# A two-layer graph attention kernel on one core: every map product as 64x64 array tiles, scores and values alternating step by step

## The chip, the core and the metric

One core of a Trainium2 chip runs the kernel. Its engines are TensorE (PE; its weight loads are shown as PEld), VectorE (DVE), ScalarE (ACT), GpSimd (POOL) and SyncE (SP), which issues most transfers. SBUF is the working memory, PSUM the accumulators that TensorE writes. The metric is the device time of one execution in microseconds; the kernel before takes 2929.03 us (median of 3 runs, 2928.76 to 2929.57).

## What is computed

Eight graphs share one adjacency matrix of 2048 x 2048 nodes; each node has 64 features. The reference, cut to its core:

```python
mask = graph + jnp.eye(N) > 0
h = jnp.einsum('bnc,hdc->bhnd', x, Wh)              # B=8, N=2048, H=4 heads of D=64
out_h = gat(h)     # scores h.h^T, masked, softmax over m, times h, plus bias bh
z = leaky_relu(concat(out_h), 0.2)
h2 = jnp.einsum('bnk,dk->bnd', z, Wo)               # 256 -> 64
out2 = gat(h2)                                      # one head, bias bo
z2 = leaky_relu(out2, 0.2)
out = layernorm(z2) * gamma + beta
return layernorm(x + out)
```

Everything is float32. The two attention layers make (32 + 8) score maps of 2048 x 2048.

## The kernel before, in words

`gat_kernel` runs `fast_kernel`, which subtracts a fixed shift in the exponent instead of a row maximum, sums all row sums into a flag, and runs `general_kernel` only if a sum left its safe range; no profile here shows the second.

`fast_kernel` works in 20 **units**. A first-layer unit (16 of them) is one batch element with two heads; a second-layer unit (4) is a pair of batch elements with the one head of layer two. In both, the two maps (j = 0, 1) lie on partitions 0-63 and 64-127 of `hT` (transposed) and in the two column halves of `hN` (plain, with the bias added). A unit has four **chunks** c of 512 columns and each chunk 16 **steps** m of 128 rows:

- `scores` (L525): for j = 0, 1 one matmul `hT[rows j, 128 of m]` x `hT[rows j, 512 of c]` into a PSUM tile of the pool "s" (L529); VectorE subtracts the mask into an SBUF tile `e` (L532), ScalarE takes the exponent in place (L534). Because the maps are symmetric, `e` holds the transposed attention.
- `values` (L537): for j = 0, 1 one matmul `hN[:, m, half j]` x `e[:, j]`, accumulated over the 16 steps in one PSUM tile `o` (L541).
- `add_up` (L544): POOL adds the `e` of steps 0 to 12 into `acc` (L550, L554); the last three (`DIRECT`) stay as they are.
- `sums` (L559): the row sums `pz` by matmuls with a vector of ones from `acc` and the three tiles, four 32-column tiles at once (L569); ScalarE copies them out (L572), transfers lay them out as `zt` (L578); the leaky relu of `o` follows on ScalarE and VectorE (L582, L583). `invert` (L586): reciprocal on VectorE, out to HBM and back as a broadcast (`rd`, `z`). `scale` (L598): `o` times `z`. `project` (L601): in layer one the product with `woT` (L608), added up over heads in `h2T`; in layer two the product with a centring matrix (L616) and `norm1`, and a period later `norm2` (L620 to L656): both layer norms, nearly all on VectorE, with the power -0.5 on POOL (L628).
- `prepare` (L498): the maps of the next unit: `ph` = `whT` x `xT` (L510), copied to `hT`, and `pn`, its transposes (L520), into `hN`.

TensorE can work as tiles: a matmul of 64 rows uses half of the rows of its array, one of 64 columns half of the columns. The score matmuls here are 64x128 tiles, two side by side; the value matmuls 128x64, two side by side; the row sums 128x32, four. A float32 matmul shows in the trace as two records.

The program order is written out by hand (`manual_schedule`): each engine runs its instructions in the order in which the loop at the end calls them. The loop goes by **periods** of four steps: `scores` four times, then the row sums if due, then `values` four times and `add_up` four times for the period before, then other jobs that the table `jobs` holds for this period (mask building, the tail of an earlier chunk, preparing the next unit). `e` tiles come from a pool of 14, "s" tiles from 3 (two PSUM banks each), `o` from 2.

Of the kernel before, what the change touches and what calls it, by code (L numbers as in the profile page):

```python
# [26 lines left out]
F32 = mybir.dt.float32  # L28
I32 = mybir.dt.int32
BF16 = mybir.dt.bfloat16  # L30
AF = mybir.ActivationFunctionType
# [5 lines left out]
SLOPE = 0.2  # L37
FMAX = 3.4028234663852886e38

BIG = 1e16  # L40
# [313 lines left out]
def fast_kernel(ctx: ExitStack, tc: tile.TileContext, x, adj, Wh, bh, Wo, bo, gamma, beta, out, flag):  # L354
# [10 lines left out]
    BATCH = 4  # L365
    K = 2 * CB
    DIRECT = 3
# [3 lines left out]
    epool = ctx.enter_context(tc.tile_pool(name="epool", bufs=14))  # L371
    accs = ctx.enter_context(tc.tile_pool(name="accs", bufs=2))
    work = ctx.enter_context(tc.tile_pool(name="work", bufs=7))
    small = ctx.enter_context(tc.tile_pool(name="small", bufs=4))
    psum = ctx.enter_context(tc.tile_pool(name="psum", bufs=3, space=bass.MemoryType.PSUM))
# [9 lines left out]
    def opsum(name):  # L385
        return psum.tile([P, W], F32, tag="o", name=name, bufs=2)

    def wtile(name):
        return work.tile([P, W], F32, tag="w", name=name)

# [5 lines left out]
    identi = const.tile([P, P], I32, name="identi")  # L396
    nc.vector.tensor_copy(identi, ident)
# [21 lines left out]
    zall = const.tile([P, chunks, 8], F32, name="zall")  # L419

# [34 lines left out]
    mask = [const.tile([P, NB, W], BF16, name=f"mask{c}") for c in range(NC)]  # L455
# [7 lines left out]
    def mask_rows(c, g, st):  # L463
        if g // 2 == c:
            for k in range(2):
                r = 2 * (g % 2) + k
                d = st[:, r, k * P:(k + 1) * P]
                nc.gpsimd.tensor_tensor(d, d, identi, OP.add)
        m = work.tile([P, CB, 2 * P], BF16, tag="w", name=f"mrow{c}_{g}")
        nc.scalar.activation(m, st, AF.Relu, bias=shifts[:, 2:3], scale=-BIG)  # L470
        return m
# [15 lines left out]

    h2T = {}

    class Unit:  # L490
# [7 lines left out]
        def prepare(self, part):  # L498

            n, h = self.n, part % 2  # L500
            if part < 2:
                if self.second:
                    self.hT = h2T[self.bp]
                    return
                if h == 0:
                    self.hT = big.tile([P, N], F32, tag="hT", name=f"hT{n}")
                rows = slice(self.b2 * C, (self.b2 + 1) * C)
                p = spsum(f"ph{n}_{h}")
                for q in range(2):
                    nc.tensor.matmul(p[:, q * W:(q + 1) * W], whT[rows, self.hp * P:(self.hp + 1) * P],  # L510
                                     xT[self.bp][rows, (2 * h + q) * W:(2 * h + q + 1) * W], start=True, stop=True)
                nc.scalar.copy(self.hT[:, h * 1024:(h + 1) * 1024], p)  # L512
                return

            if h == 0:
                self.hN = big.tile([P, NB, P], F32, tag="hN", name=f"hN{n}")
# [8 lines left out]
        def scores(self, c, m):  # L525
            ps = spsum(f"s{self.n}_{c}_{m}")
            for j in range(2):
                rows = slice(j * D, (j + 1) * D)
                nc.tensor.matmul(ps[:, j * W:(j + 1) * W], self.hT[rows, m * P:(m + 1) * P],  # L529
                                 self.hT[rows, c * W:(c + 1) * W], start=True, stop=True)  # L530
            e = slot([P, 2, W], F32, f"e{self.n}_{c}_{m}")
            nc.vector.tensor_tensor(e, ps.rearrange("p (j i) -> p j i", j=2),  # L532
                                    mask[c][:, m, :].unsqueeze(1).to_broadcast([P, 2, W]), OP.subtract)
            nc.scalar.activation(e, e, AF.Exp, bias=shifts[:, 1:2] if self.second else shifts[:, 0:1], scale=1.0)  # L534
            return e

        def values(self, c, m, e):  # L537
            if m == 0:
                self.O[c] = opsum(f"o{self.n}_{c}")
            for j in range(2):  # L540
                nc.tensor.matmul(self.O[c][j * D:(j + 1) * D, :], self.hN[:, m, j * D:(j + 1) * D], e[:, j, :],  # L541
                                 start=(m == 0), stop=(m == NB - 1))

        def add_up(self, c, m, e):  # L544
# [7 lines left out]
            elif m < NB - DIRECT:  # L552
# [4 lines left out]


        def sums(self, c):  # L559
# [20 lines left out]

            o5 = wtile(f"o5{n}_{c}")
            nc.scalar.mul(o5, self.O[c], SLOPE)  # L582
            nc.vector.tensor_tensor(self.O[c], self.O[c], o5, OP.max)  # L583
# [14 lines left out]
        def scale(self, c):  # L598
            nc.vector.tensor_tensor(self.z[c], self.O[c], self.z[c], OP.mult)  # L599

        def project(self, c):  # L601

            z, p = self.z[c], self.O[c]
            if not self.second:
                if self.bp not in h2T:
                    h2T[self.bp] = big.tile([P, N], F32, tag="h2T", name=f"h2T{self.bp}")
                rows = slice(self.b2 * D, (self.b2 + 1) * D)
                nc.tensor.matmul(p[rows, :], woT[:, self.hp, :], z, start=True, stop=True)  # L608
                dst = h2T[self.bp][rows, c * W:(c + 1) * W]
                if self.hp == 0:  # L610
                    nc.scalar.copy(dst, p[rows, :])
                else:
                    nc.vector.tensor_add(dst, dst, p[rows, :])  # L613
                return
            for i in range(CB):
                nc.tensor.matmul(p[:, i * P:(i + 1) * P], z[:, i * P:(i + 1) * P],  # L616
                                 centre.rearrange("p r d -> p (r d)"), start=True, stop=True)
            self.norm1(c, p.rearrange("p (k d) -> p k d", d=D))

        def rstd(self, c, y, tag):  # L620

            n = self.n
            st = small.tile([P, 2, K], F32, tag="st", name=f"st{n}_{c}_{tag}")
            sq = wtile(f"sq{n}_{c}_{tag}").rearrange("p (k d) -> p k d", d=D)
            nc.scalar.square(sq, y)  # L625
            nc.vector.tensor_reduce(st[:, 0, :], sq, AX.X, OP.add)  # L626
            nc.scalar.activation(st[:, 1, :], st[:, 0, :], AF.Identity, bias=shifts[:, 3:4], scale=1.0 / D)  # L627
            nc.gpsimd.tensor_tensor(st[:, 0, :], st[:, 1, :], mhalf, OP.pow)  # L628
            return st[:, 0, :].unsqueeze(2).to_broadcast([P, K, D])

        def norm1(self, c, y):
            xr = wtile(f"xr{self.n}_{c}")
            xv = xr.rearrange("p (i b d) -> p i b d", b=2, d=D)
            for b2 in range(2):
                nc.sync.dma_start(out=xv[:, :, b2, :],
                                  in_=x[2 * self.bp + b2, c * W:(c + 1) * W, :].rearrange("(i p) d -> p i d", p=P))
            nc.vector.tensor_mul(y, y, self.rstd(c, y, 0))
            nc.vector.tensor_mul(y, y, gam.unsqueeze(1).to_broadcast([P, K, D]))
            nc.vector.tensor_add(y, y, bet.unsqueeze(1).to_broadcast([P, K, D]))
            nc.vector.tensor_add(y, y, xr.rearrange("p (k d) -> p k d", d=D))  # L640
            self.xr = xr
# [156 lines left out]
```

## Time and profile before

| | |
|---|---|
| runs | 2928.76, 2929.03, 2929.57 us |
| profiled execution | 2929.27 us, span 2927.8 us |
| mean granted TensorE clock | 0.977 |
| first score matmul of unit 0 | 29.2 us after the start |
| last score matmul | 54.0 us before the end |
| busiest group on POOL | L554, 880 adds, 2079.9 us |
| chain that ended last | PE 60%, ACT 14%, DVE 11%, transfers 5% |

The page's groups give, for each line and shape, the busy time (the union of its records), the mean duration of one, and the idle time of the engine just before them with what ended it. In the order of time a row is: start, length, engine, line, operation, tiles, shape, count, and in brackets the idle time ahead of it with its releaser. In the table by stage a row is: stage, its length, then busy time and count of PE, PEld, DVE, ACT and POOL, the granted clock, the share of the DMA engines and GB/s.

### The profile page before, as it was taken

To read this page: it belongs to the slowest core of one execution; us is meant where nothing else is said; L and a number is where in the kernel's file an instruction comes from. 1 tells how busy PE (TensorE), PEld (TensorE's weight loads), DVE (VectorE), ACT (ScalarE), POOL (GpSimd) and SP (SyncE) were. 2 spreads that over 40 slices of the span, in tenths; PEclk is the share of its full clock that TensorE was granted. 3 is DMA by queue.
4 is the path that set the end of the run, shared out by engine and by line. 5 is a ranking of instruction groups with operands and counts; after the bars stand their busy time and mean duration, and the time that the engine had idled before them with its cause. 6 is when DMAs were issued, how large, how long until landed. Compare 5 with 4: busy or idle time off the path is not lost.

```text
span 2927.8 us, 33405 instructions
## 1 busy us (share of the span) xinstructions
PE 2730.6 (93%) x12550; PEld 967.9 (33%) x12550; DVE 1799.2 (61%) x1861; ACT 1656.4 (57%) x1625; POOL 2331.8 (80%) x1025
## 2 busy tenths in 40 slices
PE   7999999999998999999998899999999999998884
PEld 3333333333332333333333233333333333333221
DVE  4666656666666666566666665666566666666564
ACT  5765556556554555655654555565565556555442
POOL 5778888788777887888876888888888888877774
PEclk9999999999999999999999999999999999999997
DMA  4300001000000000100000000010000000000001
GB/s 129 123 16 8 8 8 26 8 8 8 12 22 17 10 9 8 23 8 8 12 18 12 19 8 9 8 26 8 8 8 8 8 8 12 8 12 23 15 19 27
DMA packets 118220, 54.03 MB, mean 18 GB/s; under 512 B 91266, under 2 KB 107714, under 8 KB 118050
## 3 DMA queue, kind: packets, MB, share of 16 engines
q1 hardware_dynamic: 117250, 51.36, 6.6%
q8 instruction: 100, 1.64, 0.2%
q0 software_dynamic: 176, 0.26, 0.1%
q14 instruction: 70, 0.57, 0.1%
q10 hardware_dynamic: 624, 0.20, 0.0%
HBM read 46.60 MB, written 4.52 MB: 17 GB/s over the span
## 4 chain that ended last, share of the span: by engine, by line
PE 60%; ACT 14%; DVE 11%; DMA 5%; issue 4%; SPq 3%; POOL 2%; ACTq 0%; DVEq 0%; POOLq 0%
PE o L541 28%; PE s L529 25%; ACT e L534 11%; DVE e L532 6%; DMA zt<-zsb 4%; SPq L578 3%; PE ph L510 2%; PE o L608 2%; POOL st L628 2%; ACT zsb L572 1%; PE pn L520 1%; ACT o L582 1%; PE pz L569 1%; DVE hN L522 1%; DVE st L626 1%
## 5 line engine op out<-in xcount | busy, mean ns | idle before, releaser
L554 POOL TENSOR_TENSOR acc<-acc,e 128x1024 f32<-128x1024 f32 x880 | 2079.9, 2363 | 79.5 <-ACT e L534 13.0
L534 ACT ACTIVATE e<-e,shifts 128x1024 f32<-128x1024 f32 x1280 | 1452.9, 1149 | 1034.3 <-DVE e L532 1024.6
L532 DVE TENSOR_TENSOR e<-s,mask 128x1024 f32<-128x1024 f32 x1280 | 1475.6, 1215 | 348.2 <-PE s L529 333.0
L541 PE MATMUL o<-e,hN 128*64 128x512 f32 x5120 | 1188.4, 607 | 0.0
L529 PE MATMUL s<-hT 64*128 64x512 f32 x4096 | 1004.3, 609 | 65.7 <-DVE e L532 65.7
L541 PEld LDWEIGHTS o<-e,hN 128*64 128x64 f32 x5120 | 343.5, 138 | 821.3 <-issue 600.9
L529 PEld LDWEIGHTS s<-hT 64*128 64x128 f32 x4096 | 384.1, 187 | 612.0 <-issue 308.0
L550 POOL TENSOR_TENSOR acc<-e,e 128x1024 f32<-128x1024 f32 x80 | 189.8, 2372 | 313.4 <-ACT e L534 313.4
L529 PE MATMUL s<-h2T 64*128 64x512 f32 x1024 | 261.6, 634 | 68.8 <-DVE e L532 50.6
L628 POOL TENSOR_TENSOR st<-st,mhalf 128x8 f32<-128x8 f32 x32 | 52.7, 1647 | 179.2 <-ACT st L627 179.2
L529 PEld LDWEIGHTS s<-h2T 64*128 64x128 f32 x1024 | 95.0, 192 | 215.3 <-DVE e L532 92.2
L583 DVE TENSOR_TENSOR o<-o,o 128x512 f32<-128x512 f32 x80 | 56.0, 700 | 175.8 <-ACT o L582 175.8
L569 PE MATMUL pz<-e,ones 128*32 128x512 f32 x960 | 154.1, 601 | 0.0
L589 DVE TENSOR_REDUCE zall<-zt 128x8 f32<-128x16 f32 x80 | 13.7, 171 | 199.1 <-DMA zt<-zsb 199.0
L569 PE MATMUL pz<-acc,ones 128*32 128x512 f32 x320 | 84.7, 600 | 6.2 <-POOL acc L554 2.2
L599 DVE TENSOR_TENSOR z<-o,z 128x512 f32<-128x512 f32 x80 | 55.2, 690 | 53.5 <-DMA z<-rd 53.4
L512 ACT COPY hT<-ph 128x1024 f32<-128x1024 f32 x32 | 32.4, 1012 | 82.7 <-PE ph L510 82.7
L522 DVE TENSOR_TENSOR hN<-pn,bhb 128x1024 f32<-128x1024 f32 x32 | 39.1, 1223 | 51.8 <-PE pn L520 51.8
L613 DVE TENSOR_TENSOR h2T<-h2T,o 64x512 f32<-64x512 f32 x32 | 21.9, 685 | 76.1 <-PE o L608 76.1
L510 PE MATMUL ph<-xT,whT 64*128 64x512 f32 x128 | 66.6, 644 | 0.0
L608 PE MATMUL o<-z,woT 128*64 128x512 f32 x128 | 65.5, 593 | 0.0
L626 DVE TENSOR_REDUCE st<-sq 128x8 f32<-128x512 f32 x32 | 22.0, 686 | 62.1 <-ACT sq L625 62.1
(68 smaller groups left out, 591.4 us busy)
## 6 DMA issues: line engine op xcount, KB each, us to landing
z<-rd SPq DMA_DIRECT2D x160, 128.0 KB, 2.9
adj<-in_adj_dram SPq DMA_DIRECT2D x32, 512.0 KB, 4.9
zt<-zsb SPq DMA_DIRECT2D x320, 2.0 KB, 1.8
x<-in_x_dram SPq DMA_DIRECT2D x16, 256.0 KB, 4.6
xr<-in_x_dram SPq DMA_DIRECT2D x32, 128.0 KB, 2.9
out_dram<-xr SPq DMA_DIRECT2D x32, 128.0 KB, 2.1
rd<-rt SPq DMA_DIRECT2D x80, 4.0 KB, 1.4
ws<-in_L_gnn_Wh_dram ACTq DMA_DIRECT2D x2, 64.0 KB, 4.3
```

Source lines behind the costliest of these rows:

```text
L510: nc.tensor.matmul(p[:, q * W:(q + 1) * W], whT[rows, self.hp * P:(self.hp + 1) * P], xT[self.bp][rows, (2 * h + q) * W:(2 * h + q + 1) * ...
L522: nc.vector.tensor_add(self.hN[:, h * NB // 2:(h + 1) * NB // 2, :], p.rearrange("p (m d) -> p m d", d=P), b.unsqueeze(1).to_broadcast([P, ...
L529: nc.tensor.matmul(ps[:, j * W:(j + 1) * W], self.hT[rows, m * P:(m + 1) * P], self.hT[rows, c * W:(c + 1) * W], start=True, stop=True)
L532: nc.vector.tensor_tensor(e, ps.rearrange("p (j i) -> p j i", j=2), mask[c][:, m, :].unsqueeze(1).to_broadcast([P, 2, W]), OP.subtract)
L534: nc.scalar.activation(e, e, AF.Exp, bias=shifts[:, 1:2] if self.second else shifts[:, 0:1], scale=1.0)
L541: nc.tensor.matmul(self.O[c][j * D:(j + 1) * D, :], self.hN[:, m, j * D:(j + 1) * D], e[:, j, :], start=(m == 0), stop=(m == NB - 1))
L550: nc.gpsimd.tensor_tensor(acc, self.terms[c][0], e, OP.add)
L554: nc.gpsimd.tensor_tensor(acc, acc, e, OP.add)
L569: nc.tensor.matmul(pz[q:q + 32, :W], ones, terms[s * half + k][:, j, :], start=(k == 0), stop=(k == half - 1), tile_position=(0, q))
L578: nc.sync.dma_start(out=zt[j * D:(j + 1) * D, s, :], in_=zsb[q:q + 1, :].rearrange("o (p k) -> o p k", k=8))
L608: nc.tensor.matmul(p[rows, :], woT[:, self.hp, :], z, start=True, stop=True)
L628: nc.gpsimd.tensor_tensor(st[:, 0, :], st[:, 1, :], mhalf, OP.pow)
```

## The change

- **Products as 64x64 tiles.** A score step is four matmuls (row half j, column half k), a value step four (row half r of `e`, column half j). The value sums of the two row halves go to two PSUM tiles (`O[c][0]`, `O[c][1]`), which `join` (copy on ScalarE) and `join2` (add on VectorE) bring together; `fifth` and `leaky` are the leaky relu.
- **Order.** No periods: each step t issues the scores of t, then values and `add_up` of step t - 3, then jobs. Tables give the step at which each later part of a chunk runs. Pools: "s" 2 tiles, `o` 4, `e` 13.
- **Mask** as bytes (255 or 0) instead of bf16 1e16; the diagonal is cleared after ScalarE's step, by a product on POOL.
- **Projections.** `project_x` makes the maps of both batch elements of a pair for one pair of heads at once, in four 64x64 tiles; the order of units puts both batch elements behind each other. The product with `woT` waits until both head pairs and two chunks are there (`z0` keeps the first pair) and accumulates in PSUM; ScalarE copies it to `h2T`.
- **Norms of layer two** in eight parts spread over 16 steps: sums of squares by ScalarE (`accum_out`), four 128x512 operations on POOL, two reductions on VectorE, the rest on ScalarE.
- `DIRECT` is 7 for layer two: POOL adds nine tiles instead of thirteen there, and the row sums take eight terms.

```diff
     def opsum(name):
-        return psum.tile([P, W], F32, tag="o", name=name, bufs=2)
+        return psum.tile([P, W], F32, tag="o", name=name, bufs=4)
...
+    def project_x(bp, hp, q):
+        if q == 0:
+            maps[bp, hp] = big.tile([P, 2, N], F32, tag="hT", name=f"hT{bp}_{hp}")
+        p = spsum(f"ph{bp}_{hp}_{q}").rearrange("p (b i) -> p b i", b=2)
+        for b2 in range(2):
+            rows = slice(b2 * C, (b2 + 1) * C)
+            for j in range(2):
+                nc.tensor.matmul(p[j * D:(j + 1) * D, b2, :], whT[rows, hp * P + j * D:hp * P + (j + 1) * D],
+                                 xT[bp][rows, q * W:(q + 1) * W], start=True, stop=True)
+        nc.scalar.copy(maps[bp, hp][:, :, q * W:(q + 1) * W], p)
...
         def scores(self, c, m):
-            for j in range(2):
-                rows = slice(j * D, (j + 1) * D)
-                nc.tensor.matmul(ps[:, j * W:(j + 1) * W], self.hT[rows, m * P:(m + 1) * P],
-                                 self.hT[rows, c * W:(c + 1) * W], start=True, stop=True)
+            for k in range(2):
+                for j in range(2):
+                    rows = slice(j * D, (j + 1) * D)
+                    nc.tensor.matmul(ps[k * 64:(k + 1) * 64, j, :], self.hT[rows, m * P + k * 64:m * P + (k + 1) * 64],
+                                     self.hT[rows, c * W:(c + 1) * W], start=True, stop=True)
...
         def values(self, c, m, e):
             for j in range(2):
-                nc.tensor.matmul(self.O[c][j * D:(j + 1) * D, :], self.hN[:, m, j * D:(j + 1) * D], e[:, j, :],
-                                 start=(m == 0), stop=(m == NB - 1))
+                for r in range(2):
+                    rows = slice(r * 64, (r + 1) * 64)
+                    nc.tensor.matmul(self.O[c][r][j * D:(j + 1) * D, :], self.hN[rows, m, j * D:(j + 1) * D],
+                                     e[rows, j, :], start=(m == 0), stop=(m == NB - 1))
...
+            for hp in range(HP):
+                for g in range(2):
+                    k = c - 1 + g
+                    nc.tensor.matmul(p[g * D:(g + 1) * D, :], woT[:, hp, :],
+                                     self.z[k] if hp else z0[:, self.b2, k, :], start=(hp == 0), stop=(hp == HP - 1))
...
+            if part == 1:
+                nc.vector.tensor_reduce(self.st[:, 0, :], v(self.sq), AX.X, OP.add)
+            if part == 2:
+                nc.scalar.activation(st[:, 1, :], st[:, 0, :], AF.Identity, bias=shifts[:, 3:4], scale=1.0 / D)
+                nc.gpsimd.tensor_tensor(st[:, 0, :], st[:, 1, :], mhalf, OP.pow)
+                nc.gpsimd.tensor_tensor(v(y), v(y), col(st[:, 0, :]), OP.mult)
+            elif part == 3:
+                nc.gpsimd.tensor_tensor(v(y), v(y), row(gam), OP.mult)
+                nc.gpsimd.tensor_tensor(v(y), v(y), row(bet), OP.add)
+                nc.gpsimd.tensor_tensor(y, y, xr, OP.add)
+            elif part == 4:
+                nc.vector.tensor_reduce(st[:, 2, :], v(y), AX.X, OP.add)
...
+    LATE = [(19, "join"), (20, "join2"), (20, "sums"), (21, "fifth"), (22, "leaky"), (24, "invert"), (28, "scale"), (30, "project"),
+            (31, "keep")]
+    NORM = [31, 32, 33, 35, 40, 41, 43, 46]
...
+        if 0 <= t - LAG < total:
+            u, c, m = steps[t - LAG]
+            e = es.pop(t - LAG)
+            u.values(c, m, e)
+            u.add_up(c, m, e)
```

TensorE's queue in unit 3, chunk 1, behind the row sums of chunk 0 (names are tile, unit, chunk and step; `x2` counts matmuls), before:

```order
L569 MATMUL pz3_0_3004<-e3_0_15_2924,ones_96 32x512 x2
L541 MATMUL o3_1_3023<-e3_1_0_2944,hN3_2576 64x512 x2
L541 MATMUL o3_1_3023<-e3_1_1_2950,hN3_2576 64x512 x2
L541 MATMUL o3_1_3023<-e3_1_2_2956,hN3_2576 64x512 x2
L541 MATMUL o3_1_3023<-e3_1_3_2962,hN3_2576 64x512 x2
L529 MATMUL s3_1_8_3044<-hT3_2492 128x512 x2
L529 MATMUL s3_1_9_3050<-hT3_2492 128x512 x2
L529 MATMUL s3_1_10_3056<-hT3_2492 128x512 x2
L529 MATMUL s3_1_11_3062<-hT3_2492 128x512 x2
```

And the same place in the changed kernel, where `o3_1_0` and `o3_1_1` are the two row halves' sums:

```order
L597 MATMUL pz3_0_3906<-e3_0_15_3818,ones_96 32x512 x2
L537 MATMUL s3_1_5_3922<-hT0_1_2100 64x512 x4
L550 MATMUL o3_1_0_3883<-e3_1_2_3857,hN3_3343 64x512
L550 MATMUL o3_1_1_3884<-e3_1_2_3857,hN3_3343 64x512
L550 MATMUL o3_1_0_3883<-e3_1_2_3857,hN3_3343 64x512
L550 MATMUL o3_1_1_3884<-e3_1_2_3857,hN3_3343 64x512
L537 MATMUL s3_1_6_3937<-hT0_1_2100 64x512 x4
```

Blocks of four steps have become single steps, all with 64-column outputs, and the values run three steps behind.

VectorE's queue in the second-layer unit 5, where the norms of chunk 0 stand around the scores of chunk 2, before:

```order
L626 TENSOR_REDUCE st5_0_0_4573<-sq5_0_0_4574 128x8
L637 TENSOR_TENSOR o5_0_4300<-o5_0_4300,st5_0_0_4573 128x512
L638 TENSOR_TENSOR o5_0_4300<-o5_0_4300,gam_109 128x512
L639 TENSOR_TENSOR o5_0_4300<-o5_0_4300,bet_110 128x512
L640 TENSOR_TENSOR o5_0_4300<-o5_0_4300,xr5_0_4570 128x512
L532 TENSOR_TENSOR e5_2_0_4586<-s5_2_0_4583,mask2_129 128x1024
L532 TENSOR_TENSOR e5_2_1_4592<-s5_2_1_4589,mask2_129 128x1024
L532 TENSOR_TENSOR e5_2_2_4598<-s5_2_2_4595,mask2_129 128x1024
L532 TENSOR_TENSOR e5_2_3_4604<-s5_2_3_4601,mask2_129 128x1024
L648 TENSOR_REDUCE mu5_0_4616<-o5_0_4300 128x8
L650 TENSOR_TENSOR o5_0_4300<-o5_0_4300,mu5_0_4616 128x512
L626 TENSOR_REDUCE st5_0_1_4620<-sq5_0_1_4621 128x8
```

The same stretch now, with `oj` and `o5` the copies that join and leaky read:

```order
L675 TENSOR_REDUCE st5_0_6093<-sq5_0_6076 128x8
L540 TENSOR_TENSOR e5_2_1_6100<-s5_2_1_6095,mask2_130 128x1024
L540 TENSOR_TENSOR e5_2_2_6115<-s5_2_2_6110,mask2_130 128x1024
L540 TENSOR_TENSOR e5_2_3_6127<-s5_2_3_6122,mask2_130 128x1024
L540 TENSOR_TENSOR e5_2_4_6146<-s5_2_4_6141,mask2_130 128x1024
L577 TENSOR_TENSOR o5_1_1_5873<-o5_1_1_5873,oj5_1_6139 128x512
L540 TENSOR_TENSOR e5_2_5_6185<-s5_2_5_6180,mask2_130 128x1024
L540 TENSOR_TENSOR e5_2_6_6200<-s5_2_6_6195,mask2_130 128x1024
L585 TENSOR_TENSOR o5_1_1_5873<-o5_1_1_5873,o55_1_6193 128x512
L540 TENSOR_TENSOR e5_2_7_6214<-s5_2_7_6209,mask2_130 128x1024
L540 TENSOR_TENSOR e5_2_8_6227<-s5_2_8_6222,mask2_130 128x1024
L686 TENSOR_REDUCE st5_0_6093<-y5_0_6074 128x8
```

Between the subtractions there is now never more than one operation of another kind but for the inverse; the four 128x512 operations stand on POOL, ahead of a chunk's adds (here in unit 6, which follows the second-layer unit):

```order
L563 TENSOR_TENSOR acc6_0_6742<-acc6_0_6742,e6_0_12_6889 128x1024
L679 TENSOR_TENSOR st5_3_6970<-st5_3_6970,mhalf_103 128x8
L680 TENSOR_TENSOR y5_3_6951<-y5_3_6951,st5_3_6970 128x512
L682 TENSOR_TENSOR y5_3_6951<-y5_3_6951,gam_109 128x512
L683 TENSOR_TENSOR y5_3_6951<-y5_3_6951,bet_110 128x512
L684 TENSOR_TENSOR y5_3_6951<-y5_3_6951,xr5_3_6955 128x512
L559 TENSOR_TENSOR acc6_1_7030<-e6_1_0_6963,e6_1_1_6977 128x1024
```

A chunk's norm thus delays the first add of the chunk two later, on POOL's queue, and the last two chunks of a second-layer unit do so in the unit behind it.

More of the change, by code (lines that the diff above doesn't have):

```diff
@@ L496, in __init__, with prepare @@
             self.terms, self.zt, self.z, self.O = {}, {}, {}, {}
[L498 to L513, printed above, removed]
+        def prepare(self, h):
+            n = self.n
             if h == 0:
+                self.hT = h2T[self.bp] if self.second else maps[self.bp, self.hp][:, self.b2, :]
                 self.hN = big.tile([P, NB, P], F32, tag="hN", name=f"hN{n}")
@@ L615, in project @@
[L615 to L629, printed above, removed]
```

227 lines of the change are left out of this document (126 added, 101 removed).

## The prediction

> **What bounds the kernel now.** I read the page's busy times first, then busy time by stage, then the order of time on TensorE. The stages are cut at the first score matmul of a unit: the start; unit 0, in which the mask is still being built; units 1 to 4; a second-layer unit with the unit behind it (5 and 6, then 10 and 11); units 7 to 9; 12 to 17; 18 and 19; and the tail from the last score matmul.
>
> ```profile
> PE 2730.6 (93%) x12550; PEld 967.9 (33%) x12550; DVE 1799.2 (61%) x1861; ACT 1656.4 (57%) x1625; POOL 2331.8 (80%) x1025
> ...
> 0.00:29.20 29.20, 17.17 (x62) 10.63 (x62) 3.85 (x10) 8.45 (x8) 5.52 (x21) 1.00 0.75 201
> 29.20:182.20 153.00, 144.95 (x817) 58.70 (x816) 102.56 (x110) 108.94 (x103) 118.38 (x60) 0.99 0.28 88
> 182.20:724.10 541.90, 530.41 (x2441) 186.01 (x2440) 336.85 (x336) 319.32 (x304) 453.31 (x192) 1.00 0.04 11
> 724.10:1032.10 308.00, 279.72 (x1243) 98.06 (x1242) 190.93 (x202) 165.67 (x170) 239.90 (x105) 0.96 0.06 15
> 1032.10:1438.80 406.70, 397.57 (x1835) 139.48 (x1834) 252.60 (x252) 239.43 (x228) 340.53 (x145) 1.00 0.05 11
> 1438.80:1745.80 307.00, 277.75 (x1243) 97.68 (x1242) 190.91 (x202) 165.87 (x170) 239.79 (x105) 0.96 0.06 15
> 1745.80:2560.20 814.40, 796.54 (x3659) 279.09 (x3658) 504.98 (x504) 479.21 (x456) 681.03 (x289) 1.00 0.04 10
> 2560.20:2873.80 313.60, 272.21 (x1203) 92.69 (x1202) 197.72 (x216) 160.70 (x171) 237.83 (x106) 0.94 0.08 19
> 2873.80:2927.80 54.00, 14.30 (x70) 5.55 (x66) 18.76 (x31) 8.85 (x16) 15.54 (x8) 0.64 0.09 21
> ```
>
> In a first-layer unit (541.9 / 4 = 135.5 us) the second column, PE, is busy 98% of the stage and nothing else comes near it: TensorE sets the time. A pair with a second-layer unit takes 308 us, 37 more than two first-layer units, its PE busy share falls to 91%, and the granted clock (behind the counts) to 0.96. So there are two things to win: TensorE's own work, and the second layer's holes.
>
> ```profile
> 908.87 3.65 PE L541 MATMUL o<-e,hN 128*64 128x512 f32 x16
> 912.45 3.70 PE L529 MATMUL s<-hT 64*128 64x512 f32 x16
> 916.09 3.65 PE L541 MATMUL o<-e,hN 128*64 128x512 f32 x16
> ...
> 900.62 0.14 PEld L541 LDWEIGHTS o<-e,hN 128*64 128x64 f32 x2 [0.28 <-issue]
> 901.05 0.14 PEld L541 LDWEIGHTS o<-e,hN 128*64 128x64 f32 x2 [0.29 <-issue]
> ```
>
> An f32 matmul is two records. In a block of 16, pairs of weight loads come every 0.43 us: two tiles run side by side and a slot lasts 0.43. Eight slots are 3.44 us, yet blocks start 3.58 and 3.64 us apart, so a switch between the 64x128 tiles of the scores and the 128x64 tiles of the values costs about 0.18 us: eight in a chunk (16 steps), 640 in all, 115 us.
>
> ```profile
> L569 PE MATMUL pz<-e,ones 128*32 128x512 f32 x960 | 154.1, 601 | 0.0
> L510 PE MATMUL ph<-xT,whT 64*128 64x512 f32 x128 | 66.6, 644 | 0.0
> L608 PE MATMUL o<-z,woT 128*64 128x512 f32 x128 | 65.5, 593 | 0.0
> L520 PE MATMUL pn<-ident,hT 128*128 128x128 f32 x256 | 35.5, 284 | 0.0
> L616 PE MATMUL o<-centre,z 128*128 128x128 f32 x128 | 19.5, 298 | 14.2 <-DVE z L599 14.2
> ...
> 940.31 0.62 PE L569 MATMUL pz<-acc,ones 128*32 128x512 f32 x2
> 940.33 0.62 PE L569 MATMUL pz<-e,ones 128*32 128x512 f32 x2
> 940.74 0.62 PE L569 MATMUL pz<-acc,ones 128*32 128x512 f32 x2
> 940.78 1.46 PE L569 MATMUL pz<-e,ones 128*32 128x512 f32 x10
> 942.17 3.65 PE L541 MATMUL o<-e,hN 128*64 128x512 f32 x16
> ```
>
> With these prices a chunk of before comes to 27.5 (64 slots) + 1.4 (switches) + 1.95 (row sums) + 1.2 (projection 65.5/64 and a switch) + 0.6 (value transposes, 35.5/64) + 1.1 (input projection, 66.6/64) = 33.8 us; measured 541.9/16 = 33.9. The prices hold.
>
> **The change, part by part.** *Map products.* Each step now has four 64x64 tiles twice, one after the other in one mode. The row-sum block is the nearest thing in this trace: four tiles (two of acc, two of e) start within 0.02 us of each other, their second passes 0.43 us later, and 16 records end in 1.86 us. So four at once cost one slot. Bounds: 0.43 (these four) and 0.86 (two at a time, as now); I take 0.43, since scores already use two row tiles side by side, values two column tiles and row sums four column tiles, each at 0.43. A step is then 4 slots = 1.72 us as before; the gain is the 640 switches, not the tiles. The other blocks still switch.
>
> *First-layer chunk now:* 27.5 + row sums 1.86 and a switch = 2.1 + transposes (1.1 and two switches, twice a unit) 0.75 + input projection (four tiles of 0.43, two passes, two chunks a unit) 0.43 + output projection (four slots and two switches, once a unit) 0.53 = 31.3 us; a unit 125.2 instead of 135.5. *Second-layer chunk:* 27.5 + row sums of eight terms, 8 slots and two switches, 3.8 + centring 19.5/16 and two switches 1.6 + 0.75 = 33.7; a unit 134.6.
>
> ```profile
> L554 POOL TENSOR_TENSOR acc<-acc,e 128x1024 f32<-128x1024 f32 x880 | 2079.9, 2363 | 79.5 <-ACT e L534 13.0 <-PE s L529 0.7
> L532 DVE TENSOR_TENSOR e<-s,mask 128x1024 f32<-128x1024 f32 x1280 | 1475.6, 1215 | 348.2 <-PE s L529 333.0 <-POOL acc L554 12.1 <-issue 3.0
> L534 ACT ACTIVATE e<-e,shifts 128x1024 f32<-128x1024 f32 x1280 | 1452.9, 1149 | 1034.3 <-DVE e L532 1024.6 <-ACT e L534 0.9 <-issue 0.3
> L628 POOL TENSOR_TENSOR st<-st,mhalf 128x8 f32<-128x8 f32 x32 | 52.7, 1647 | 179.2 <-ACT st L627 179.2
> L468 POOL TENSOR_TENSOR adj<-adj,identi 128x128 int32<-128x128 int32 x16 | 7.0, 458 | 11.1 <-DMA adj<-in_adj_dram 11.1
> 357.99 19.45 POOL L554 TENSOR_TENSOR acc<-acc,e 128x1024 f32<-128x1024 f32 x8
> ```
>
> *The cover.* Eight adds in a row take 19.45, 2.43 each: twelve in a first-layer chunk are 29.2 us on POOL, beside 29.6 (27.5 + 2.1) of TensorE in a chunk without other work. POOL is now as good as level with it; it hides by 0.4 us there and by 2 on the mean. VectorE (1.215) and ScalarE (1.149) fit a step of 1.72, with 0.5 to spare. The score buffers go from three to two: a score ends 0.86 into its step, its subtraction about 2.3 in, and the buffer is wanted at 3.44; 1.1 us of slack. The new join and leaky operations (two of 0.70 on VectorE, two of 0.6 on ScalarE a chunk) fit the spare 0.5 of two steps.
>
> *The second layer's norms.* Today they stand in VectorE's queue:
>
> ```profile
> 924.27 0.70 DVE L637 TENSOR_TENSOR o<-o,st 128x512 f32<-128x512 f32 x1 [2.09 <-POOL st L628]
> 928.35 2.08 PE L529 MATMUL s<-hT 64*128 64x512 f32 x4 [4.74 <-DVE e L532]
> ```
>
> VectorE waits for the power on POOL and then runs four 0.70 us operations, with the next subtractions queued behind; TensorE sits 4.74 us for one of these. In the change only two reductions are left on VectorE; four 128x512 operations go to POOL. The trace has none of that shape: 0.458 (128x128) and 2.363 (128x1024) bound it, the line through both gives 1.27. With two powers of 1.65, a small one of 0.2 and gaps it is 9 us a chunk. A second-layer chunk has only 8 adds (19.4), so 28.5 hides under 33.7. But the norms of the last two chunks fall into the next unit, where POOL then needs 2 x (29.2 + 9) = 76 us against about 63 of TensorE: I charge 13 us, twice (behind units 5 and 10). The sixteen small ScalarE operations a chunk (bounds 0.19 and 0.60, the 128x8 and 128x512 ones) cost 4 to 5 us of ScalarE, some 25 of 33.7 in all: hidden, though they come in bursts. The byte mask (VectorE bounds 0.69 and 1.22, its shortest and longest 128x1024 operations) hides under the step at either end.
>
> ```profile
> 2894.07 1.78 DMA zt<-zsb
> 2896.40 1.44 DMA rd<-rt
> 2898.36 3.01 DMA z<-rd
> 2914.13 1.65 POOL st L628
> ```
>
> *Moved waits.* Row sums to inverse have 4 steps, inverse to scale 4 steps = 6.9 us; of that the two transfers take 1.44 and 3.01, the small work and issues around them under 1. SP's queue has no load or store of the norms between them.
>
> ```profile
> 2884.80 0.65 PE L569 MATMUL pz<-acc,ones 128*32 128x512 f32 x2 [2.20 <-POOL acc L554]
> ```
>
> *Tail and start.* Today the last row sums wait for POOL until 11 us after the last score; with eight adds instead of twelve about 5. The norm chain behind is some 3 us longer (four times 1.27 for 0.70, and small ScalarE operations): I put the tail at 48 for 54. The start makes both batch elements' maps, but in four tiles: 30 for 29.2.
>
> *The sum:* start 30, unit 0 125.2 + 17.5 (153.0 over 135.5, its mask work) = 143, units 1-4 501, 5 and 6 134.6 + 125.2 + 13 = 273, 7-9 376, 10 and 11 273, 12-17 752, 18 and 19 267, tail 48: **2663 us of span** against 2927.8. The profiled execution took 2929.27, 1.5 over its span, and lies at the runs' median of 2929.03: so 2664.
>
> **The rivals.** *A, the switch stays.* The 0.18 us may come from going over to other operands and another output, not from the tile shape; alternating by step then makes 2560 of them: 2664 + 2560 x 0.18 = **3125**, slower. It decides from 265/2560 = 0.10 us a switch. Against it: inside a block the step changes weights, operand and semaphore with no gap. For it: no row shows scores behind values in one shape. 6%.
>
> *B, weight loads that no longer hide.* Two of the four tiles share their rows, and if a load had to wait for the neighbour's matmul, each of 5120 slots would grow by a load's 0.14: 2664 + 707 = **3370**; it decides from 0.05 a slot. Against it, the value rows above: both tiles there use all 128 rows, the loads take 0.14 and the slot stays 0.43. With it goes the case of four tiles that run two at a time, 5120 x 0.43 more, 4865. Together 5%. The Trainium skill has this rule in "TensorE: Matmul & The Clock Gate", Part 3: a weight load overlaps matmuls in flight only where its row group differs. By that rule this change would lose; the value and row-sum rows of this trace disagree with it.
>
> *C, waits in the queues eat part of it.* Each chunk now has two VectorE operations behind a ScalarE one, where one today waits long:
>
> ```profile
> L583 DVE TENSOR_TENSOR o<-o,o 128x512 f32<-128x512 f32 x80 | 56.0, 700 | 175.8 <-ACT o L582 175.8
> ```
>
> That is 2.2 us each. If both still waited so, 2.2 + 0.7 less 0.6 spare and 1.1 slack is 1.2 us of TensorE, 160 times: 2664 + 190 = **2855**, still faster. POOL level with TensorE, or bursts on ScalarE, would show alike; half of it is 2760. Against it: join and join2 stand a step apart in program order, leaky a step behind its product. 14%.
>
> **How the numbers follow.** The forecast, 2664, has 74%, its own range 2600 (switches around the other blocks hidden too, no charge for POOL) to 2725. Rival C reaches 2855, A and B beyond 3100, and 1% remains. The range 2600 to 2830 holds the forecast and most of C, about 85%. Faster by over 0.2%, which is about what a measurement of this kernel can tell from no change: 0.87; within: 0.01; slower: 0.12, mostly A and B.
>
> **What would show it.** Right: score and value records four to a slot of 0.43 in an unbroken run of blocks; first-layer units near 125; pairs behind a second-layer unit near 273 and a clock of 1.00 there. A shows as gaps of 0.1 us or more at each turn from scores to values; B as slots over 0.48; C as TensorE waiting for the subtraction (scores) or for POOL's sum (row sums) in most chunks. I would be wrong above all if four 64x64 tiles behave unlike four 128x32 ones.

## The result, and the profile after

The changed kernel takes **2678.84 us** (median of 4 runs, 2678.67 to 2681.78) against 2929.3 us (2928.76 to 2931.13): a ratio of 0.9146, with a 95% interval of 0.913 to 0.9162. The forecast was 2664 us, 15 less. The profiled execution has a span of 2677.1 us at a mean granted clock of 0.985.

The page's busy times of the changed kernel, and its busy time by stage, cut as in the prediction (columns as there):

```profile
PE 2580.8 (96%) x23174; PEld 896.5 (33%) x23174; DVE 1832.5 (68%) x1797; ACT 1783.3 (67%) x2089; POOL 2265.1 (85%) x1041
...
0.00:28.70 28.70, 15.51 (x88) 9.23 (x88) 5.18 (x10) 10.38 (x10) 5.43 (x21) 0.94 0.81 217
28.70:169.10 140.40, 138.36 (x1305) 51.66 (x1308) 121.58 (x112) 106.63 (x101) 111.13 (x57) 1.00 0.30 93
169.10:669.70 500.60, 500.09 (x4536) 172.23 (x4532) 355.32 (x345) 332.44 (x323) 458.76 (x195) 1.00 0.05 12
669.70:945.80 276.10, 262.26 (x2342) 90.15 (x2338) 181.14 (x181) 187.47 (x273) 222.39 (x109) 0.98 0.07 17
945.80:1321.70 375.90, 375.64 (x3400) 129.52 (x3396) 266.49 (x259) 248.98 (x243) 341.24 (x145) 1.00 0.05 13
1321.70:1597.70 276.00, 262.19 (x2340) 90.15 (x2336) 181.30 (x181) 187.44 (x273) 222.30 (x109) 0.98 0.07 17
1597.70:2345.00 747.30, 746.78 (x6766) 257.24 (x6761) 533.06 (x517) 494.86 (x481) 682.56 (x289) 1.00 0.05 12
2345.00:2623.20 278.20, 267.19 (x2361) 92.03 (x2357) 180.11 (x182) 194.85 (x321) 201.29 (x106) 0.98 0.08 20
2623.20:2677.10 53.90, 12.76 (x82) 4.31 (x74) 8.28 (x16) 20.27 (x71) 19.98 (x17) 0.62 0.13 31
```

| stage | before | forecast | measured |
|---|---|---|---|
| start | 29.2 | 30 | 28.7 |
| unit 0 | 153.0 | 143 | 140.4 |
| units 1 to 4 | 541.9 | 501 | 500.6 |
| units 5 and 6 | 308.0 | 273 | 276.1 |
| units 7 to 9 | 406.7 | 376 | 375.9 |
| units 10 and 11 | 307.0 | 273 | 276.0 |
| units 12 to 17 | 814.4 | 752 | 747.3 |
| units 18 and 19 | 313.6 | 267 | 278.2 |
| tail | 54.0 | 48 | 53.9 |

In the first-layer stages behind unit 0 TensorE is now busy 99.9% (500.09 of 500.60 in units 1 to 4). Units 1 to 4 and 7 to 9 came out as forecast, unit 0 and units 12 to 17 are 3 and 5 us shorter. What is above the forecast, by 3, 3, 11 and 6, lies in the stages with a second-layer unit and in the tail, and only those show a granted clock below 1.00 behind the start.

TensorE and its weight loads in unit 6 of the changed kernel, in the order of time:

```profile
872.59 1.04 PE L537 MATMUL s<-hT 64*64 64x512 f32 x8
872.59 0.15 PEld L537 LDWEIGHTS s<-hT 64*64 64x64 f32 x4 [0.28 <-issue]
873.02 0.15 PEld L550 LDWEIGHTS o<-e,hN 64*64 64x64 f32 x4 [0.28 <-issue]
873.44 1.04 PE L550 MATMUL o<-e,hN 64*64 64x512 f32 x8
873.45 0.15 PEld L550 LDWEIGHTS o<-e,hN 64*64 64x64 f32 x4 [0.28 <-issue]
```

Scores start at 872.59 and the values behind them at 873.44: 0.85 for eight records, four to a slot of 0.43, with no gap at the turn. All four weight loads of a slot fit in 0.15 and hide.

The two groups of projections of the changed kernel, by line, count and busy time:

```profile
L506 PE MATMUL ph<-xT,whT 64*64 64x512 f32 x256 | 34.9, 622 | 0.3 <-ACT hT L508 0.3
L641 PE MATMUL o<-z,woT 128*64 128x512 f32 x128 | 31.0, 605 | 0.0
```

Both are about half of before (66.6 and 65.5). Of the 250.7 us by which the span shrinks, 98.3 came in the three stages with second-layer units and 151.8 in those with first-layer units alone. The 640 switches at 0.18 are an estimated 115 of the whole, the shorter projections some 66; no run takes back the projections, the byte mask or the pools alone, so the remainder is not shared out among them.

The rest of the story is in the waits of the changed kernel (engine and line, what it waited for; us in total, times, longest):

```profile
ACT xr L698 <- POOL st L695: 42.8, 13, 6.3
PE o L550 <- ACT e L541: 20.1, 7, 4.9
PE s L537 <- DVE e L540: 20.1, 10, 3.9
```

One such place in unit 6, in the order of time:

```profile
863.22 12.14 POOL L563 TENSOR_TENSOR acc<-acc,e 128x1024 f32<-128x1024 f32 x5
875.33 1.65 POOL L694 TENSOR_TENSOR st<-st,mhalf 128x8 f32<-128x8 f32 x1
877.29 2.76 ACT L698 ACTIVATE xr<-y,st 128x64 f32<-128x64 f32 x8 [6.34 <-POOL st L695]
879.95 3.21 ACT L541 ACTIVATE e<-e,shifts 128x1024 f32<-128x1024 f32 x3
881.14 1.56 PE L550 MATMUL o<-e,hN 64*64 64x512 f32 x8 [4.94 <-ACT e L541]
884.11 1.98 PE L537 MATMUL s<-hT 64*64 64x512 f32 x8 [1.42 <-ACT hT L508]
885.87 1.93 PE L550 MATMUL o<-e,hN 64*64 64x512 f32 x8
```

GpSimd works through a chunk's adds, of which the first row shows the last five, before it reaches the second power of the norm (L694). The norm's last part on ScalarE (L698) is already at the head of its queue and waits 6.34 us for it; the exponents are queued behind it, and TensorE waits 4.94 for the first of them. Then two slots take 1.76 (884.11 to 885.87) instead of 0.86: behind this hole TensorE runs at half clock for a few microseconds (the granted clock is 0.50 from 881.7 to 888.4).

The same wait in unit 5 takes another way:

```profile
765.97 2.76 ACT L698 ACTIVATE xr<-y,st 128x64 f32<-128x64 f32 x8 [2.99 <-POOL st L695]
770.14 0.59 ACT L665 ACTIVATE sq<-o 128x512 f32<-128x512 f32 x1
770.76 0.69 DVE L675 TENSOR_REDUCE st<-sq 128x8 f32<-128x512 f32 x1 [4.22 <-ACT sq L665]
771.36 1.22 DVE L540 TENSOR_TENSOR e<-s,mask 128x1024 f32<-128x1024 f32 x1
772.63 1.98 PE L537 MATMUL s<-h2T 64*64 64x512 f32 x8 [3.85 <-DVE e L540]
```

ScalarE's wait makes the next chunk's squares late; VectorE, whose reduction of them stands ahead of a subtraction, waits for them; and TensorE waits 3.85 for that subtraction. Three queues pass one wait on.

### The profile page after: what moved, and what is told of

Its sections match the earlier page's. It is cut to its first block, busy times and chain, and to the rows that moved or that the text cites. A ratio compares the mean times of both kernels' runs of the same rounds, so it can differ in the third digit from the quotient of the medians.

```text
span 2677.1 us, 54824 instructions
## 1 busy us (share of the span) xinstructions
PE 2580.8 (96%) x23174; PEld 896.5 (33%) x23174; DVE 1832.5 (68%) x1797; ACT 1783.3 (67%) x2089; POOL 2265.1 (85%) x1041
## 4 chain that ended last, share of the span: by engine, by line
PE 76%; POOL 11%; ACT 6%; DVE 3%; issue 3%; DMA 0%; SPq 0%; POOLq 0%; DVEq 0%; ACTq 0%
PE s L537 34%; PE o L550 33%; POOL acc L563 6%; PE pz L597 5%; ACT e L541 3%; DVE e L540 2%; PE pn L527 1%; ACT xr L698 1%; PE o L641 1%; ACT xr L690 1%; POOL acc L559 1%; POOL st L694 1%; POOL st L679 1%; ACT hT L508 1%; PE pm L484 1%
## 5 line engine op out<-in xcount | busy, mean ns | idle before, releaser
L540 DVE TENSOR_TENSOR e<-s,mask 128x1024 f32<-128x1024 f32 x1280 | 1562.6, 1222 | 721.7 <-PE s L537 700.3
L563 POOL TENSOR_TENSOR acc<-acc,e 128x1024 f32<-128x1024 f32 x816 | 1933.5, 2369 | 81.2 <-ACT e L541 20.2
L550 PE MATMUL o<-e,hN 64*64 64x512 f32 x10240 | 1336.6, 592 | 20.2 <-ACT e L541 20.1
L537 PE MATMUL s<-hT 64*64 64x512 f32 x8192 | 1074.3, 595 | 9.6 <-DVE e L540 4.5
L550 PEld LDWEIGHTS o<-e,hN 64*64 64x64 f32 x10240 | 390.9, 134 | 738.6 <-issue 540.7
L537 PEld LDWEIGHTS s<-hT 64*64 64x64 f32 x8192 | 295.8, 133 | 582.2 <-issue 424.9
L537 PE MATMUL s<-h2T 64*64 64x512 f32 x2048 | 273.1, 604 | 15.7 <-DVE e L540 15.6
L537 PEld LDWEIGHTS s<-h2T 64*64 64x64 f32 x2048 | 75.2, 135 | 157.9 <-issue 121.3
L600 ACT COPY zsb<-pz 128x512 f32<-128x512 f32 x80 | 46.7, 584 | 48.3 <-PE pz L597 48.3
L698 ACT ACTIVATE xr<-y,st 128x64 f32<-128x64 f32 x128 | 44.1, 426 | 42.8 <-POOL st L695 42.8
L577 DVE TENSOR_TENSOR o<-o,oj 128x512 f32<-128x512 f32 x80 | 55.9, 698 | 2.4 <-ACT oj L572 1.0
```

The lines of the kernel that those rows point to most:

```text
L537: nc.tensor.matmul(ps[k * 64:(k + 1) * 64, j, :], self.hT[rows, m * P + k * 64:m * P + (k + 1) * 64], self.hT[rows, c * W:(c + 1) * W], st ...
L540: nc.vector.tensor_tensor(e, ps, mask[c][:, m, :].unsqueeze(1).to_broadcast([P, 2, W]), OP.subtract)
L550: nc.tensor.matmul(self.O[c][r][j * D:(j + 1) * D, :], self.hN[rows, m, j * D:(j + 1) * D], e[rows, j, :], start=(m == 0), stop=(m == NB - 1))
L563: nc.gpsimd.tensor_tensor(acc, acc, e, OP.add)
L577: nc.vector.tensor_tensor(b, b, self.t, OP.add)
L698: nc.scalar.activation(v(xr)[:, k, :], v(y)[:, k, :], AF.Identity, bias=st[:, 1, k:k + 1], scale=st[:, 0, k:k + 1])
```

## The experiments

The theory after the result: the map products cost what the forecast says, and the miss is ScalarE's queue behind GpSimd's late power, with the half clock behind the holes. All edits are made on the changed kernel, and all kernels below compute the whole result.

### One part undone: scores back as two 64x128 tiles

```diff
-            for k in range(2):
-                for j in range(2):
-                    ... ps[k * 64:(k + 1) * 64, j, :], hT[rows, 64 columns of m] ...
+            for j in range(2):
+                ... ps[:, j, :], hT[rows, 128 columns of m] ...
```

> The scores alone go back to two 64x128 tiles; the step-by-step order, the values and all else stay as in the changed kernel. Theory (the tile form costs the switch): each of 1280 steps now has two switches of 0.18 us, 2560 in all, about 460 us on top of 2679, so near 3140, and a step of 2.08 us instead of 1.716. Rival (the switch was not the form, but the going over between blocks of four): a step stays at 1.72 and the time near 2680.

Measured: 3041.16 us (one run). TensorE in unit 1 of this kernel, in the order of time:

```profile
201.24 1.13 PE L536 MATMUL s<-hT 64*128 64x512 f32 x4
202.30 1.09 PE L549 MATMUL o<-e,hN 64*64 64x512 f32 x8
203.32 1.13 PE L536 MATMUL s<-hT 64*128 64x512 f32 x4
```

A step takes 2.08 us (201.24 to 203.32) where it takes 1.72 with one shape: the same four slots and two switches of 0.18. The chunk without other work goes from 29.5 to 35.1 us, 5.6 over 31 new switches, 0.18 each (of the 32 turns between scores and values one holds the row sums, whose two switches were there before). So the switch is one of tile shape, and rival A falls. The total grew by 362, not 460: chunks with other work on TensorE grew by 3.3 to 5.5, since a switch or two at such work was there already, and the three that held the holes of a pair by -4.4 to 1.6. With more time on TensorE, GpSimd keeps up: ScalarE's wait for the power is 4.1 us in this run instead of 42.8. The kernel is 4% slower than before although the number of slots is the same: alternating by step pays only with equal shapes.

### The norms in one lump

All eight parts of a norm are put at step 31.

```diff
-    NORM = [31, 32, 33, 35, 40, 41, 43, 46]
+    NORM = [31, 31, 31, 31, 31, 31, 31, 31]
```

> All eight parts of a norm stand in one piece at step 31 instead of over 16 steps; the operations and their engines are the same. Theory (the spreading is what took the second layer's holes away): each of 16 chunks blocks VectorE and ScalarE for a chain of some 18 us, of which the score buffers and the lag of three steps hide about 3 to 5, so 13 to 15 us each, 210 to 240 in all: near 2900, with TensorE at 1.0 in first-layer units as before. Rival (that POOL took the work from VectorE is what counts, the order is not): under 30 us more, near 2700.

Measured: 2858.94 us (one run). A chunk beside a norm takes 45.8 to 50.2 us, where these chunks take 32.5 to 41.4 in the changed kernel; first-layer units without a norm beside them stay as they are. Unit 5 of this kernel, in the order of time:

```profile
734.92 1.67 POOL L679 TENSOR_TENSOR st<-st,mhalf 128x8 f32<-128x8 f32 x1 [10.65 <-ACT st L678]
741.76 0.69 DVE L686 TENSOR_REDUCE st<-y 128x8 f32<-128x512 f32 x1 [7.26 <-POOL y L684]
743.64 1.98 PE L537 MATMUL s<-h2T 64*64 64x512 f32 x8 [9.07 <-DVE e L540]
```

The norm's chain from power to second reduction takes 7 us, and VectorE and ScalarE stand in it with the subtractions and exponents behind them. Against this lump the spreading is worth 180 us, 11 a chunk where the theory had 13 to 15.

### The power earlier, or the end of the norm later

Two ways to take the wait out of ScalarE's queue: the power's step from 43 to 41, or the last part's step from 46 to 53, with a fourth `y` buffer, five instead of six of the other work tiles, and a record of `y`, `xr` and `st` for each chunk.

```diff
-    NORM = [31, 32, 33, 35, 40, 41, 43, 46]
+    NORM = [31, 32, 33, 35, 40, 41, 41, 46]
```

> The second power of a norm and the small product behind it go two steps up in POOL's queue (step 41 instead of 43), ahead of two adds of 2.43 us; nothing else is moved. Theory (ScalarE's last part waits 3.0 to 6.3 us for them, and the exponents behind it hold up the values): 4.9 us earlier takes nearly all of these waits away, 43 us in the changed kernel; TensorE's holes after them, 40 in the stream and 4 in the tail, shrink to those where the row sums wait for POOL (about 5 twice, as in the run with the later end): 2640 to 2655. Rival (POOL's load in these chunks): no more than 10 off, 2669 or above.

```diff
-    NORM = [31, 32, 33, 35, 40, 41, 43, 46]
+    NORM = [31, 32, 33, 35, 40, 41, 43, 53]
```

> The last part of a norm (eight small ScalarE operations and the store) runs at step 53 instead of 46, with one more buffer for it and one work buffer less. Theory (POOL is late with the power behind its adds, and ScalarE, which stands in line for it, holds up the exponents): the holes of TensorE in the second-layer units, the unit behind them and in the tail go, 46 us in the changed kernel with the tail's, so 2635 to 2645; ScalarE waits for POOL's small product near 0 instead of 43 us. Rival (POOL's work in those chunks, 76 against 63 us, sets their time whatever stands where): the holes move to the row sums that wait for POOL, and the time stays within 10 us of 2679.

Measured: the power earlier 2649.3 us (2647.37 to 2651.43), ratio to before 0.9039 [0.9024, 0.9054]; the end later 2669.13 us (2665.99 to 2669.39), 0.9101 [0.9086, 0.9117]. The waits and stages of the kernel with the power earlier (pairs 5 and 6, 10 and 11, units 18 and 19, tail):

```profile
ACT xr L698 <- POOL st L695: 5.8, 3, 2.0
PE pz L597 <- POOL acc L563: 12.9, 4, 4.0
...
670.30:939.40 269.10, 258.35 (x2340) 89.49 (x2336) 181.14 (x181) 187.66 (x273) 222.42 (x109) 1.00 0.07 17
1315.70:1586.60 270.90, 261.53 (x2344) 89.77 (x2340) 181.31 (x181) 187.80 (x273) 222.59 (x109) 0.99 0.07 17
2333.80:2598.10 264.30, 262.09 (x2360) 91.06 (x2356) 180.02 (x182) 195.02 (x321) 201.65 (x107) 1.00 0.08 21
2598.10:2646.40 48.30, 10.10 (x82) 3.93 (x74) 8.28 (x16) 20.09 (x71) 19.57 (x16) 0.64 0.14 35
```

ScalarE's wait falls from 42.8 to 5.8 us. The stages lose 7.0, 5.1, 13.9 and 5.6, together 31.6, where the span shrinks by 30.7 (2677.1 to 2646.4), and the clock is back at 0.99 to 1.00. That is the miss of the prediction, in the four places where it lay. What is new is the second row: with the first wait gone, row sums wait for GpSimd's adds.

The end later takes the same wait away (2.0 us are left) and gains a third as much. That is outside the theory's 2635 to 2645, and just inside the 10 us that the rival allowed. The wait that the rival named, of row sums for GpSimd, is there (10.1 us), but it is 12.9 beside the earlier power, so it doesn't explain the 20 us between the two. The second row below is the new one:

```profile
PE pz L597 <- POOL acc L563: 10.1, 4, 4.6
DVE o L585 <- ACT o L581: 38.8, 14, 5.3
```

The eight operations now come in a step in which ScalarE also has the next chunk's late parts, and VectorE's leaky relu waits for those, up to 5.3 us with subtractions behind it.

### GpSimd's load behind the second-layer units

Seven of eight terms of the row sums straight from the exponents (or five of six) instead of three of four, in chunks 0 and 1 of units 6 and 11: alone, with the end later, and with the power earlier. The edit for seven:

```diff
-            elif m < NB - DIRECT[self.second]:
+            elif m < NB - DIRECT[self.second or (c < 2 and self.n in (6, 11))]:
```

> In the first two chunks of the two first-layer units that follow a second-layer unit POOL adds nine tiles instead of thirteen, and the row sums take eight terms. Both theories say that POOL's load falls by 9.7 us in each of these four chunks, and TensorE gets 4 slots more (1.7 us). If POOL's load sets these chunks, units 6 and 11 lose 2 x (19 - 3.4) = 31 us at most; if only the place of the power in POOL's queue matters, they lose the holes in them, 2 x 10.7, less 2 x 3.4 = 15: near 2664. The holes inside the second-layer units themselves stay under both.

> The later last part (step 53) and the shorter POOL sums in the first two chunks of units 6 and 11 together. In the run with the later end the row sums of chunk 1 there waited 4.7 us for POOL, with TensorE at half clock behind it; with four adds fewer that wait goes, 2 x (4.7 + 2.5), against 4 x 1.7 for the longer row sums: 8 us below that run's 2669, near 2661. If POOL's load were not behind that wait, it stays and the time is near 2676. The pile-up on ScalarE at steps 4 to 9 (holes of 1.7 us a second-layer chunk) stays under both.

> The power one step pair earlier, and in chunks 0 and 1 of units 6 and 11 the row sums take seven of their eight terms straight from the exponents. Theory (what is left of the loss behind the second-layer units is GpSimd's load in those chunks, two holes of 2.6 and 4.2 us in which row sums wait for its adds, with some 3 us of half clock after each pair): the waits go, about 13.5 + 4 us, and the four chunks pay four more row-sum terms each, 4 x 1.7 = 6.9 us: 2640 us, between 2636 and 2644. Rival (the load only shifts to a later chunk): 2650 to 2657, no better than the power alone.

> As the run before, but five terms straight from the exponents: GpSimd is spared two adds of 2.43 us in a chunk (4.9 us, 9.8 us in a pair of chunks), and row sums pay two terms more, 4 x 0.86 = 3.4 us. Theory: holes of 6.8 us in a pair are covered by 9.8 us, so the time is that of the power alone less 17 and plus 3.4: 2636 us, between 2634 and 2642. Rival (too little relief, the first hole stays): 2645 to 2652.

| kernel | us | ratio to before, 95% interval |
|---|---|---|
| seven, alone | 2680.53 (2677.44 to 2681.22) | 0.914 [0.9125, 0.9155] |
| seven, end later | 2658.33 (2656.92 to 2659.97) | 0.9067 [0.9052, 0.9082] |
| seven, power earlier | 2636.45 (2635.52 to 2637.96) | 0.8996 [0.8981, 0.9011] |
| five, power earlier | **2633.31** (2633.22 to 2635.57) | 0.8984 [0.8969, 0.8999] |

Alone, less load on GpSimd gains nothing, where 15 us were expected. Its queue in unit 6 of that kernel:

```profile
849.27 1.64 POOL L679 TENSOR_TENSOR st<-st,mhalf 128x8 f32<-128x8 f32 x1 [8.10 <-ACT st L678]
875.53 1.65 POOL L694 TENSOR_TENSOR st<-st,mhalf 128x8 f32<-128x8 f32 x1
```

The second power of a norm comes behind the adds of steps 0 to 8 of its chunk, and those that are spared are the later ones, of steps 9 to 12. So GpSimd rests 8.10 us ahead of the next norm, whose input isn't there yet, and the power starts at 875.53 where it started at 875.33. ScalarE still waits 34.1 us in this kernel, and the row sums are longer.

Behind the earlier power seven terms gain 12.9 us and five 16.0, and behind the later end seven gain 10.8; these three came within 4 us of what was expected. Units 5 and 6 of the last kernel, five terms and the power earlier:

```profile
671.80:934.10 262.30, 259.73 (x2356) 90.16 (x2352) 181.27 (x181) 187.71 (x273) 213.20 (x105) 1.00 0.07 18
```

TensorE is busy 99% of it, and the other pair takes 262.7. From 270.0 (mean of 269.1 and 270.9) a pair falls to 262.5, and 1.7 of that it pays for the added terms (four slots of 0.43): GpSimd's load had cost 9.2 us a pair. Seven terms say nearly the same: 264.0 a pair, 3.4 of it for added terms, so 9.4. This kernel beats the changed one by 45.5 us, 1.7%.

### Three terms in the second layer too

```diff
-    DIRECT = (3, 7)
+    DIRECT = (3, 3)
```

> Row sums take three terms straight from the exponents in second-layer chunks as well, so GpSimd makes 12 adds of 2.43 us and the four operations of the norm, 29.2 + 9 = 38 us, in a chunk in which TensorE has 32.5 less 1.7. Theory (GpSimd's load is the next bound there): each of 16 chunks becomes 38 us or more, 16 x 5.7 = 91 us and holes, 2770 to 2790 us. Rival (GpSimd still hides): 16 x 1.7 = 27 us less, 2652.

Measured: 2686.37 us (one run), as good as level with 2678.84, which neither expected. Busy time by stage of this kernel, units 5 and 6:

```profile
671.20:947.70 276.50, 260.10 (x2276) 89.11 (x2272) 181.42 (x181) 187.73 (x273) 260.19 (x125) 0.96 0.07 17
```

GpSimd (fifth column) is busy 260 of 276.5 us: nearly full, not over. My 38 us a chunk counted a norm beside every chunk, but a norm comes two chunks behind its own, and the adds of unit 6 carry none in its later chunks; the load is to be summed over the pair. Two chunks of unit 5 get shorter by 1.7 and 1.5 us, as eight slots become four, and holes behind them give it back. ScalarE's wait for the power is there too (60.2 us), so this run doesn't tell how much of it is GpSimd's load.

### The four norm operations on VectorE

```diff
-                nc.gpsimd.tensor_tensor(v(y), v(y), col(st[:, 0, :]), OP.mult)
+                nc.vector.tensor_tensor(v(y), v(y), col(st[:, 0, :]), OP.mult)
...
-                nc.gpsimd.tensor_tensor(y, y, xr, OP.add)
+                nc.vector.tensor_tensor(y, y, xr, OP.add)
```

> The four 128x512 operations of a norm run on VectorE at the same steps; POOL keeps the powers. POOL loses 4.9 us in each of 16 chunks, VectorE gets 2.8. Theory (POOL's lateness is what makes the holes): ScalarE's waits for POOL and the holes behind them go, 40 to 45 us; against that the three operations in one step (2.1 us) pass the slack of 1.1 us that VectorE has before TensorE waits for a score buffer, about 0.5 to 1 us in 16 chunks, and the power's wait now stands in VectorE's queue, 1.65 us where POOL is free: 2645 to 2670. Rival (VectorE was the engine that had to be freed): most of what before lost in its second-layer chunks comes back, over 2700.

Measured: 2742.25 us (2741.27 to 2745.67), 0.9359 [0.9343, 0.9374]: 63 slower than the changed kernel, and where the rival had it. The theory was wrong by its price for VectorE. First unit 5 and then the tail of this kernel, in the order of time:

```profile
739.63 2.33 POOL L559 TENSOR_TENSOR acc<-e,e 128x1024 f32<-128x1024 f32 x1
739.68 2.83 DVE L680 TENSOR_TENSOR y<-y,st 128x512 f32<-128x512 f32 x1 [3.15 <-POOL st L679]
743.70 1.49 PE L537 MATMUL s<-h2T 64*64 64x512 f32 x8 [4.81 <-DVE e L540]
745.03 5.34 POOL L563 TENSOR_TENSOR acc<-acc,e 128x1024 f32<-128x1024 f32 x2 [3.08 <-ACT e L541]
745.41 2.73 DVE L683 TENSOR_TENSOR y<-y,bet 128x512 f32<-128x512 f32 x1
748.17 2.75 DVE L684 TENSOR_TENSOR y<-y,xr 128x512 f32<-128x512 f32 x1
...
2701.16 0.69 DVE L680 TENSOR_TENSOR y<-y,st 128x512 f32<-128x512 f32 x1 [2.08 <-POOL st L679]
```

The operation takes 0.69 us in the tail, where GpSimd rests, and 2.83 beside an add of 2.33: it ends some 0.5 us after the add does. TensorE waits 4.81 for the subtraction behind it. All but the two in the tail of the 16 operations at L680 take 2.81 to 2.83. The four operations on VectorE before took 0.70 each, three of them with an add beside them from end to end; there one operand was in PSUM, here both are in SBUF.

## Why the prediction was right, point by point

- **A slot of four 64x64 tiles, 0.43:** right (872.59 to 873.44 is two of them). Units 1 to 4 take 125.15 each against 125.2.
- **The switch, 640 x 0.18:** right in size (0.18 again) and in cause, by the kernel with 64x128 scores. Rival A falls with it.
- **Weight loads (rival B):** the rows above have four loads in 0.15 beside a slot. The rule of the Trainium skill in "TensorE: Matmul & The Clock Gate", Part 3, that a load overlaps only where the row group differs, disagrees: two of the four tiles share their rows, and the slot stays 0.43.
- **Rival C:** the joins and leaky relus cost TensorE nothing in first-layer units. Waits in queues did come, but of another kind: 20.1 + 20.1 us in all, and only around norms.
- **GpSimd's 13 us behind units 5 and 10:** a term of the right kind, mis-sized and at first masked. It measured 9.2 us a pair, by what the lighter load gained once the other wait was out of the way; in the changed kernel itself no matmul of the row sums waits for GpSimd, since the stalls ahead of them gave it time.
- **The step that failed** is "The sixteen small ScalarE operations a chunk ... hidden, though they come in bursts". Their own time (2.76 us for the last eight) was hidden. But I costed ScalarE by its load, and not by what its queue waits for: the last eight stand three steps (5.2 us) behind a power that GpSimd starts only when its add in hand and those queued ahead are done, at 2.4 us each. That cost 31 us: 7 and 5 in the pairs, 14 in units 18 and 19, where six of the eight chunks have a norm beside them (four in a pair), and 6 in the tail.
- **The tail, 48:** 53.9, and 48.3 with the power earlier; its excess is the same wait.
- **A hit with some luck.** Without that wait the kernel has a span of 2646.4 against the forecast's 2663. So the forecast was 17 too high elsewhere: 4 and 2 in the pairs, 5 in units 12 to 17, 3 each in unit 0 and units 18 and 19. For units 18 and 19 the sum has 267, though its own two units of 134.6 make 269.2; it gives no reason for the 2 us less. The wait of 31 and this 17 of the other sign make the 14 us by which the span missed (2677.1 against 2663).

## What to carry to other kernels

Where an engine switches between tile shapes, count the switches: here one cost 0.18 us, and by that price one shape for all neighbours saved 115 us without saving a slot. When work is spread over the queues of several engines, check for each part not only whether its engine has time, but when its input leaves the queue of the engine ahead, and put at least the longest stretch of that queue between the two, at a place where the waiting engine has nothing else in a burst: the end moved later freed ScalarE of the one wait and made others. After removing a wait look at the trace again: the lighter load on GpSimd gained nothing alone and 12.9 us once ScalarE no longer waited.

## What the runs showed of the hardware

- **VectorE and GpSimd get in each other's way.** Beside GpSimd's adds a VectorE operation with both operands in SBUF took 2.8 us instead of 0.69. The Trainium skill states it in "SBUF — State Buffer", section "SBUF: two separate sides": a pair of ports is shared, and of a VectorE operation with two SBUF inputs and a GpSimd operation that reads SBUF the one that starts first holds it to its end. The trace agrees: the operation above ends 0.5 us behind the add that had started first.
- **Half clock after holes.** In the changed kernel seven stretches of 2.6 to 5.3 us, 29.5 us in all, have slots of 0.86 instead of 0.43 at a granted clock of 0.50, each behind one hole (3.85 and 4.94 above) or, once, two of under 2 us close together: some 15 us lost on top of the holes. The length of a hole alone doesn't decide it here. The two short holes stand at three more places (behind 843, 1495 and 2594 us) without half clock after them, and in the kernel with the power earlier a hole of 4.00 was not followed by it, while one of 4.02 at the same place of the other pair (1529 us) was. The rows of the first, with the next slot 0.45 later:

```profile
883.55 0.62 PE L597 MATMUL pz<-acc,ones 128*32 128x512 f32 x2 [4.00 <-POOL acc L563]
884.00 0.60 PE L597 MATMUL pz<-acc,ones 128*32 128x512 f32 x2
```
